# Layer 2's depthwise units: norms with an operand in PSUM, a fourth convolution bank, a sixth half buffer, gate nets in pieces

## The chip, the cores and the metric

The kernel runs on one core of a Trainium2 chip. The metric is the device time of one execution in microseconds, as a median of several runs. The profile that is read here is one further execution, traced instruction by instruction. Engines are called as the profile calls them: PE (TensorE matmul), PEld (its weight load), DVE (VectorE), ACT (ScalarE), POOL (GpSimd), SP (SyncE, here only a DMA queue).

## The reference

The input is x of shape (4, 384, 64, 64), fp32. Four layers follow each other, each as `x = x + layer(groupnorm(x))`: an attention over 96 of the channels, a Fourier filter with a 3x3 depthwise convolution, a re-parametrised depthwise block with a channel MLP, and a 7x7 depthwise convolution with kernels made from the data. The change lies in the third, called layer 2:

```python
p = x.mean(axis=(2, 3), keepdims=True)
h = _gelu(_bn(_pw(p, dc_w1), dc_g1, dc_b1))
decision = jax.nn.sigmoid(_bn(_pw(h, dc_w2), dc_g2, dc_b2))
gate = jax.nn.sigmoid((decision - 0.5) / 1.0)
a = _gelu(_bn(_pw(p, kp_w1), kp_g1, kp_b1))
kw = jax.nn.softmax(_bn(_pw(a, kp_w2), kp_g2, kp_b2), axis=1)
y3 = _bn(_dw(x, c3_w, 1), c3_g, c3_b)
y5 = _bn(_dw(x, c5_w, 2), c5_g, c5_b)
y1 = x * c1_w + c1_b
tok = _bn(kw[:, 0:1] * y3 + kw[:, 1:2] * y5 + y1, ar_g, ar_b)
gp = tok.mean(axis=(2, 3), keepdims=True)
gh = _gelu(_bn(_pw(gp, cg_w1), cg_g1, cg_b1))
gates = jax.nn.sigmoid(_bn(_pw(gh, cg_w2), cg_g2, cg_b2))
tok = tok * gates
h1 = _gelu(_bn(_pw(tok, cm_w1), cm_g1, cm_b1))
h2 = _bn(_pw(h1, cm_w2), cm_g2, cm_b2)
return gate * (tok + h2) + (1.0 - gate) * x
```

`_bn` takes mean and variance over batch and space, `_dw` is a depthwise and `_pw` a 1x1 convolution.

## The kernel before

A tile framework orders the instructions of each engine by its own priorities, gives out the buffers of each pool, and sets the waits. The order in the program text is therefore only roughly the order on an engine, but each engine works through its own list strictly in order.

Layers 0 and 1 run first. Their output x1 goes to DRAM. Then `phase_b` computes the token stage of layer 2 (up to `tok` before its norm), `phase_ef` the gates and the channel MLP, and `phase_g` layer 3.

`phase_b` works in twelve **units** of 32 channels each, with 4 batches x 32 channels on the 128 partitions. A group of four units shares one block of 128 channels of z, the strips of x1 in transposed form: a strip is two image rows (128 positions on the partitions). For each unit:

- `matrices53` makes the banded matrices of the 5x5 and 3x3 convolution for two channels, as a product of taps `w` with a 0/1 band (L1103, tile `toep`, four buffers). Odd ones are made on POOL, with the band in SBUF, and even ones on DVE, with the band in PSUM (`band7_p`).
- `conv53` does the convolution of two channels as six matmuls into one PSUM bank `conv_m` (L1122, three banks). ACT copies it to `d_o` (L1131), DVE takes statistics (L1134), and after every four the ACT queue stores `d_o` to DRAM. There are sixteen of these per unit.
- `conv_norms` turns the statistics into scale and shift of the two batch norms, joined with the branch weights `k_u`: a matmul `cn_rep` for the mean over partitions, small DVE steps for the variance, matmuls `cn_m`, a root as Ln and Exp on ACT (two activation tables), and then some fifteen small DVE steps. It leaves the scales `cn_s`, a shift, and `about`, the point around which squares are summed later.
- `unit_tok` of the unit before runs in the same loop: `c_d` brings the stored convolutions back from DRAM in the other layout, ACT writes `x * c1_w + shift` to the PSUM bank `tok_m` (L1209, two banks), DVE adds the 3x3 and the 5x5 branch (L1212, L1214), ACT sums the squares (L1219), and the SP queue stores `tok`. This is done in four chunks of two halves.
- `unit_strips` of the next unit loads its x1 (`unit_x`, pool `b_x`, two half buffers per unit, five in all), normalises it on ACT (L1044), and, from the second group of four on, transposes it on PE (`strip_m`, L1051) and copies it into z. The first group's strips are made by `strips5`, during layer 1 and at the start of `phase_b`; the last four use `b_x` as well.

Before the units, `nets` computes the gate and the two branch weights from pooled x: two tiny matmuls, each followed by a batch norm over four values (`bn_of_four`: statistics on DVE, Ln and Exp on ACT, three small DVE steps of `bn_scale_shift` at L321 to L323, an activation), and a last pair of matmuls `net_m`. Its instructions are issued before the loop:

```python
self.units(cp)
self.nets(cp)
self.unit_x = [[] for _ in range(UNITS)]
for _ in self.unit_strips(0):
    pass
```

At its start `phase_ef` computes the channel gates, for each of three channel blocks a matmul `cg_z` and a `bn_of_four` with a sigmoid, and then the factors `at` and `ct` that scale every `e_tok` tile ahead of the MLP's first matmul `h_s` (L1342).

PSUM in `phase_b` before: two banks `m` for small results, transposes and `cn_` tiles, one for the band, three `c` for `conv_m`, two `t` for `tok_m`.

Of the kernel before, what the change touches and what calls it, by code (L numbers as in the profile page):

```python
# [39 lines left out]
UNITS = C // 32  # L40
# [185 lines left out]
class _Builder:  # L226
# [728 lines left out]
    def phase_b(self):  # L955

        tc, nc = self.tc, self.nc  # L960
        with ExitStack() as ctx:
            self.open_psum(ctx, 2)
            cp = ctx.enter_context(tc.tile_pool(name="b_const", bufs=1))
            self.bx_p = ctx.enter_context(tc.tile_pool(name="b_x", bufs=5))
            self.bt_p = ctx.enter_context(tc.tile_pool(name="b_t", bufs=2))
            self.bc_p = ctx.enter_context(tc.tile_pool(name="b_c", bufs=3))
            self.band7 = self.const(cp, "band7")
            self.band7_p = self.psum.tile([P, 512], F32, tag="band", name="band7_p", bufs=1)[:, 0:W]
            nc.vector.tensor_copy(self.band7_p, self.band7)
# [12 lines left out]
            for _ in self.unit_strips(0):  # L982
                pass
            for u in range(UNITS):
                st = self.bt_p.tile([P, 2, 16, 6], F32, tag="st", name="st")
                strips = self.unit_strips(u + 1) if u + 1 < UNITS else iter(())
                tok = self.unit_tok(u - 1) if u else iter(())
                for n in range(16):
                    self.matrices53(16 * u + n + 2)
                    self.conv53(u, n, st)  # L990
                    next(strips if n % 2 else tok, None)
                self.conv_norms(u, st)
            for _ in self.unit_tok(UNITS - 1):
                pass
            self.tok_stats()

    def units(self, pool):

        nc = self.nc
        self.norm_u = pool.tile([P, 3, UNITS], F32, tag="norm_u", name="norm_u")  # L1000
        self.same32 = self.const(pool, "same32")
        self.swap(
            self.norm_u.rearrange("p k (j q) -> p (k j) q", q=4), self.norm2.rearrange("p k j b -> p (k j) b")
        )

# [3 lines left out]
        self.k_u, self.about = tile_of("k_u", 2), tile_of("about", UNITS)  # L1009
# [101 lines left out]
    def conv53(self, u, n, st):  # L1111

        nc = self.nc
        c0 = u % 4 * 32 + 2 * n
        t = self.toep.pop(16 * u + n)
        if n % 4 == 0:
            self.d_o = self.bt_p.tile([P, 2, 8, P], F32, tag="d_o", name="d_o")
        m = self.psum.tile([P, 512], F32, tag="c", name="conv_m", bufs=3)
        for c in range(2):
            for i in range(3):  # L1120
                at = (c0 + c) * 132 + 4 * i
                nc.tensor.matmul(  # L1122
                    m[:, c * 256 : (c + 1) * 256],
                    lhsT=self.z_[:, at : at + P],
                    rhs=t[:, 12 * c + 4 * i : 12 * c + 4 * i + 4].rearrange("p m a n -> p (m a n)"),
                    start=i == 0,
                    stop=i == 2,
# [14 lines left out]
    def conv_norms(self, u, st):  # L1142


        nc = self.nc
        at = slice(u, u + 1)
        parts = st.rearrange("p v n (e s) -> p (v n e) s", e=2)
        rep = self.pm("cn_rep")
        nc.tensor.matmul(rep[:, 0:64], lhsT=self.mean128, rhs=parts[:, :, 1], start=True, stop=True)
# [23 lines left out]
        c = self.sm([P, 2], "cn_c")  # L1173
        s = self.sm([P, 2], "cn_s")
        for v, k in enumerate(("c5", "c3")):
            nc.vector.tensor_mul(a[:, v : v + 1], a[:, v : v + 1], self.vec(f"{k}_g")[:, at])
        nc.vector.tensor_mul(c, mean, a)
        s0 = self.sm([P, 1], "cn_s0")
        nc.vector.tensor_copy(s0, self.vec("c1_b")[:, at])
        for v, k in enumerate(("c5", "c3")):  # L1180
            nc.vector.tensor_sub(c[:, v : v + 1], self.vec(f"{k}_b")[:, at], c[:, v : v + 1])
            nc.vector.scalar_tensor_tensor(s0, c[:, v : v + 1], self.k_u[:, v : v + 1], s0, ALU.mult, ALU.add)
        nc.vector.tensor_mul(s, a, self.k_u)

        about = self.about[:, at]
        nc.vector.tensor_add(about, self.c1_u[:, at], s0)
        nc.vector.tensor_mul(mean, mean, s)
        for v in range(2):
            nc.vector.tensor_add(about, about, mean[:, v : v + 1])
        nc.vector.tensor_scalar(about, about, -1.0, None, ALU.mult)  # L1190
        self.tok_s = s, s0

    def unit_tok(self, u):
# [4 lines left out]
        for i in range(4):  # L1198
# [40 lines left out]
    def nets(self, cp):  # L1239
# [8 lines left out]
            nc.tensor.matmul(z[0:12, 0:B], lhsT=w1[:, j, :], rhs=self.p2[:, j, :], start=j == 0, stop=j == NJ - 1)  # L1248
        hid = self.sm([12, B], "net_h")
        self.bn_of_four("net1", z[0:12, 0:B], self.vec("net_g1", 12), self.vec("net_b1", 12), AF.Gelu, hid)  # L1250
        z = self.pm("net_z2")
        nc.tensor.matmul(z[0:3, 0:B], lhsT=w2, rhs=hid, start=True, stop=True)
        z2 = self.sm([3, B], "net_z2s")
        self.bn_of_four("net2", z[0:3, 0:B], self.vec("net_g2", 3), self.vec("net_b2", 3), AF.Identity, z2)

        m = self.pm("net_m")
        nc.tensor.matmul(m[:, 0:B], lhsT=net[:, 0:P], rhs=z2, start=True, stop=True)
# [10 lines left out]
        for v, k in enumerate((self.k5, self.k3)):  # L1268
            nc.vector.tensor_mul(own, k, self.vec("batch"))
            nc.vector.tensor_reduce(self.k_u[:, v : v + 1], own, AX.X, ALU.add)  # L1270

    def phase_ef(self):
        tc, nc = self.tc, self.nc
        with ExitStack() as ctx:
# [30 lines left out]

# [479 lines left out]
```

## Time and profile before

| | |
|---|---|
| time, median of 3 | 5168.03 us (5156.67 to 5169.5) |
| span of the profiled run | 5165.3 us, mean granted clock 0.947 |
| PE busy | 4669.4 us, 90% |
| DVE busy | 2742.2 us, 53% |
| ACT busy | 2093.9 us, 41% |
| POOL busy | 734.3 us, 14% |
| first to last matmul of L1122 | 2628.4 to 3258 us |
| first matmul of the MLP, `h_s` | 3311.0 us |

A group row of the profile gives busy time, the mean of one instruction, and the idle time before it with what ended it. The view of waits says which instruction waited for which, in total. The view of stretches gives the busy time of every engine between two times, the granted clock (1.00 is full speed), the share of the 16 DMA engines and the rate. The timeline lists instructions in order of time, with the idle time ahead of each in square brackets. Every fp32 matmul appears as two records.

### The profile page before, as it was taken

How to read it: one execution, taken by the hardware profiler on the slowest of the kernel's cores; microseconds unless marked ns; L12 is line 12 of the kernel's file. 1: busy time of each engine (PE TensorE's matmuls, PEld its weight loads, DVE VectorE, ACT ScalarE, POOL GpSimd, SP SyncE). 2: the span in 40 equal slices, each digit the busy share in tenths (PEclk: the TensorE clock that was granted, in tenths of full speed). 3: DMA queues.
4: the chain of work that ended last, by engine and by line, in shares of the span. 5: the costliest groups of instructions: out<-in, count | busy, mean ns of one | idle time of the engine just before them, and what ended most of it. 6: DMA issues, size and time to landing. Idle time of an engine off the chain costs nothing. (4 is left out here: it accounts for less than half of the span.)

```text
span 5165.3 us, 48069 instructions
## 1 busy us (share of the span) xinstructions
PE 4669.4 (90%) x17963; PEld 2579.1 (50%) x17963; DVE 2742.2 (53%) x4606; ACT 2093.9 (41%) x2736; POOL 734.3 (14%) x524
## 2 busy tenths in 40 slices
PE   5999999999999999999878999599999995549999
PEld 2333444334443343435457777344444442449999
DVE  4322456634565345566768888644431113657775
ACT  3544344454444444433135555411133334652320
POOL 1000000000000000000035555100000000125433
PEclk9999999999999999999979999799999997659999
DMA  5210211111121111112158999766644434647776
GB/s 157 74 48 28 88 56 67 55 54 45 49 74 66 36 37 63 66 68 93 65 161 259 271 279 278 250 242 240 250 175 164 155 134 173 225 169 245 228 223 190
DMA packets 387543, 723.30 MB, mean 140 GB/s; under 512 B 21627, under 2 KB 221158, under 8 KB 380390
## 3 DMA queue, kind: packets, MB, share of 16 engines
q1 hardware_dynamic: 333528, 519.50, 32.4%
q10 hardware_dynamic: 28494, 105.99, 5.2%
q0 software_dynamic: 25280, 94.65, 4.7%
q8 instruction: 145, 2.38, 0.2%
q14 instruction: 96, 0.79, 0.0%
HBM read 432.48 MB, written 287.57 MB: 139 GB/s over the span
## 5 line engine op out<-in xcount | busy, mean ns | idle before, releaser
L734 PE MATMUL av<-probs,vt 128*97 128x512 f32 x2048 | 962.2, 605 | 0.0
L703 ACT ACTIVATE probs<-sc_s 128x1024 f32<-128x1024 f32 x512 | 499.5, 1021 | 756.6 <-PE av L734 739.5
L734 PEld LDWEIGHTS av<-probs,vt 128*97 128x97 f32 x2048 | 322.1, 166 | 507.7 <-issue 504.3
L1122 PE MATMUL conv_m<-toep,z 128*128 128x256 f32 x2304 | 527.4, 389 | 33.5 <-ACT d_o L1131 17.6
L918 DVE SCALAR_TENSOR_TENSOR acc<-band,vecs,acc 128x512 f32<-128x512 f32 x696 | 493.1, 746 | 42.6 <-POOL band L879 25.0
L1391 PE MATMUL h_m<-f_h,cm_w_t 128*128 128x512 f32 x1152 | 496.2, 594 | 7.9 <-ACT f_h L1381 7.9
L1122 PEld LDWEIGHTS conv_m<-toep,z 128*128 128x128 f32 x2304 | 443.0, 195 | 98.9 <-issue 17.7
L1103 POOL TENSOR_TENSOR toep<-w,band 128x1536 f32<-128x1536 f32 x96 | 330.4, 3442 | 313.3 <-PE conv_m L1122 254.3
L1342 PE MATMUL h_s<-e_tok,cm_w_t 128*128 128x512 f32 x768 | 366.4, 601 | 5.1 <-DVE e_tok L1327 5.1
L1675 PE MATMUL conv_m<-toep,z 128*128 128x128 f32 x3072 | 364.7, 277 | 1.9 <-DVE rest_o L1683 1.9
L1391 PEld LDWEIGHTS h_m<-f_h,cm_w_t 128*128 128x128 f32 x1152 | 219.7, 191 | 284.4 <-issue 271.7
L1675 PEld LDWEIGHTS conv_m<-toep,z 128*128 128x128 f32 x3072 | 355.7, 194 | 2.4 <-issue 2.1
L695 PE MATMUL sc_s<-q,k 32*128 32x512 f32 x2048 | 300.8, 644 | 16.3 <-ACT probs L703 11.5
L841 PE MATMUL t_m<-w_in_t,xb 128*128 128x384 f32 x768 | 283.6, 503 | 7.6 <-DVE coef L858 3.3
L767 PE MATMUL proj_m<-xm,w_proj_t 128*128 128x512 f32 x576 | 265.8, 600 | 0.8 <-DVE xm L720 0.8
L1349 ACT COPY e_h<-h_s 128x1024 f32<-128x1024 f32 x96 | 97.2, 1012 | 415.8 <-PE h_s L1342 415.8
L774 DVE SCALAR_TENSOR_TENSOR x_res<-proj_m,bn_c,x_res 128x512 f32<-128x512 f32 x96 | 71.8, 748 | 338.0 <-PE proj_m L767 338.0
L1342 PEld LDWEIGHTS h_s<-e_tok,cm_w_t 128*128 128x128 f32 x768 | 148.2, 193 | 191.9 <-issue 185.5
L1351 DVE BATCH_NORM_STATS2 h_st<-e_h 128x6 f32<-128x512 f32 x192 | 123.4, 685 | 203.7 <-ACT e_h L1349 203.7
L1399 DVE BATCH_NORM_STATS2 h_st<-f_h 128x6 f32<-128x512 f32 x72 | 50.0, 694 | 322.8 <-ACT f_h L1398 322.8
L841 PEld LDWEIGHTS t_m<-w_in_t,xb 128*128 128x128 f32 x768 | 142.3, 193 | 151.0 <-issue 66.3
L1342 PE MATMUL h_s<-z,cm_w_t 128*128 128x512 f32 x384 | 198.3, 600 | 12.6 <-DVE z L1327 12.6
(366 smaller groups left out, 6322.5 us busy)
## 6 DMA issues: line engine op xcount, KB each, us to landing
d<-d_o ACTq DMA_DIRECT2D x96, 512.0 KB
c_d<-d SPq DMA_DIRECT2D x96, 512.0 KB
hid<-e_h ACTq DMA_DIRECT2D x16, 3072.0 KB
f_h<-hid SPq DMA_DIRECT2D x16, 3072.0 KB
x_res<-in_x SPq DMA_DIRECT2D x32, 768.0 KB
x_in<-in_x SPq DMA_DIRECT2D x96, 256.0 KB
xa<-x_res POOLq DMA_DIRECT2D x32, 768.0 KB, 3.9
xa_in<-xa SPq DMA_DIRECT2D x32, 768.0 KB
```

Source lines behind the costliest of these rows:

```text
L695: nc.tensor.matmul(s[:, g], lhsT=k4[32 * g : 32 * g + 32, c], rhs=q[i][32 * g : 32 * g + 32], start=True, stop=True,)
L703: nc.scalar.activation(p[:, h * 1024 : (h + 1) * 1024], s[:, 2 * h : 2 * h + 2].rearrange("p a b -> p (a b)"), AF.Exp, scale=0.25,)
L734: nc.tensor.matmul(av[0 : PD + 1, :], lhsT=vt[:, 4 * c + v, :], rhs=p[:, v * 512 : (v + 1) * 512], start=c == 0 and v == 0, stop=c == 7 an ...
L767: nc.tensor.matmul(m, lhsT=self.w_proj[:, j, o * P : (o + 1) * P], rhs=xm[:, j], start=j == 0, stop=j == NJ - 1,)
L841: nc.tensor.matmul(m[:, 0:C], lhsT=xb[:, j], rhs=self.w_in[:, j, :], start=j == 0, stop=j == NJ - 1,)
L918: nc.vector.scalar_tensor_tensor(out, src(j, k), w, done, ALU.mult, ALU.add)
L1103: eng.tensor_tensor(t, self.w53[:, at : at + 192].rearrange("p (m n) -> p m n", n=8).unsqueeze(2).to_broadcast([P, 24, 8, 8]), band.rearra ...
L1122: nc.tensor.matmul(m[:, c * 256 : (c + 1) * 256], lhsT=self.z_[:, at : at + P], rhs=t[:, 12 * c + 4 * i : 12 * c + 4 * i + 4].rearrange("p ...
L1342: nc.tensor.matmul(s[:, v, :], lhsT=w1[:, j, o * P : (o + 1) * P], rhs=t[j][:, v * 512 : (v + 1) * 512], start=j == 0, stop=j == NJ - 1,)
L1351: nc.vector.bn_stats(st[:, o, 8 * b + 2 * i + v, :], h[:, o, v * 512 : (v + 1) * 512])
L1391: nc.tensor.matmul(m, lhsT=w2[:, o, j * P : (j + 1) * P], rhs=h[:, o, v * 512 : (v + 1) * 512], start=o == 0, stop=o == 5,)
L1675: nc.tensor.matmul(m[:, ch * P : (ch + 1) * P], lhsT=self.z_[:, at : at + P], rhs=t[:, 8 * c + 2 * i : 8 * c + 2 * i + 2].rearrange("p m a ...
```

## The change

Five things change, all in layer 2:

1. `conv_norms`: the mean and its deviation stay in PSUM (`rep`, `m`), so that each two-input DVE step has at most one operand in SBUF. A copy (`cn_four`) and a square go to ACT. The products of gains and biases with the branch weights, for all units at once, are made in `nets` (`gk`, `base`), as is `about`, which needs no convolution statistics after all since the means cancel. The small DVE steps from the root to the shift and to `about`, some fifteen, become four.
2. `conv_m` gets four banks, `tok_m` one. The last unit's `tok_m` uses the four `c` banks, which are free then.
3. `b_x` gets a sixth half buffer.
4. `nets` becomes a generator in pieces, taken up after the third, sixth and ninth convolution of unit 0, and unit 0's own `unit_strips` moves into that loop.
5. The gates of `phase_ef` are normed for all three channel blocks together, with one root.

```diff
-            self.bx_p = ctx.enter_context(tc.tile_pool(name="b_x", bufs=5))
+            self.bx_p = ctx.enter_context(tc.tile_pool(name="b_x", bufs=6))
...
-            self.nets(cp)
             self.unit_x = [[] for _ in range(UNITS)]
-            for _ in self.unit_strips(0):
-                pass
...
-                tok = self.unit_tok(u - 1) if u else iter(())
+                tok = self.unit_tok(u - 1) if u else self.unit_strips(0)
+                nets = iter(()) if u else self.nets(cp)
                 for n in range(16):
                     self.matrices53(16 * u + n + 2)
                     self.conv53(u, n, st)
                     next(strips if n % 2 else tok, None)
+                    if n % 3 == 2:
+                        next(nets, None)
...
-        m = self.psum.tile([P, 512], F32, tag="c", name="conv_m", bufs=3)
+        m = self.psum.tile([P, 512], F32, tag="c", name="conv_m", bufs=4)
...
-        rep = self.pm("cn_rep")
-        nc.tensor.matmul(rep[:, 0:64], lhsT=self.mean128, rhs=parts[:, :, 1], start=True, stop=True)
-        d = self.sm([P, 64], "cn_d")
-        nc.vector.tensor_sub(d, parts[:, :, 1], rep[:, 0:64])
-        nc.vector.tensor_mul(d, d, d)
-        nc.vector.scalar_tensor_tensor(d, parts[:, :, 2], 1.0 / P, d, ALU.mult, ALU.add)
...
-        nc.vector.tensor_copy(four[:, 0], spread(parts[:, :, 1]))
+        nc.scalar.copy(four[:, 0], spread(parts[:, :, 1]))
+        rep = self.pm("cn_rep")
+        mean, d = rep[:, 0:64], rep[:, 64:128]
+        nc.tensor.matmul(mean, lhsT=self.mean128, rhs=parts[:, :, 1], start=True, stop=True)
+        nc.vector.tensor_sub(d, parts[:, :, 1], mean)
+        nc.scalar.activation(d, d, AF.Square)
+        nc.vector.scalar_tensor_tensor(d, parts[:, :, 2], 1.0 / P, d, ALU.mult, ALU.add)
...
-        mean = self.sm([P, 2], "cn_mean")
-        nc.vector.tensor_copy(mean, m[:, 0:2])
-        a = self.sm([P, 2], "cn_a")
-        self.rsqrt(a, m[:, 2:4])
...
-        about = self.about[:, at]
-        nc.vector.tensor_add(about, self.c1_u[:, at], s0)
-        nc.vector.tensor_mul(mean, mean, s)
-        for v in range(2):
-            nc.vector.tensor_add(about, about, mean[:, v : v + 1])
-        nc.vector.tensor_scalar(about, about, -1.0, None, ALU.mult)
+        self.rsqrt(m[:, 4:6], m[:, 2:4])
+        nc.vector.tensor_mul(s, m[:, 4:6], self.gk[:, u])
+        nc.vector.tensor_mul(m[:, 6:8], m[:, 0:2], s)
+        nc.vector.scalar_tensor_tensor(s0, m[:, 6:7], -1.0, self.base[:, u : u + 1], ALU.mult, ALU.add)
+        nc.vector.scalar_tensor_tensor(s0, m[:, 7:8], -1.0, s0, ALU.mult, ALU.add)
...
-                m = self.psum.tile([P, 512], F32, tag="t", name="tok_m", bufs=2)
+                last = u == UNITS - 1
+                m = self.psum.tile([P, 512], F32, tag="c" if last else "t", name="tok_m", bufs=4 if last else 1)
...
+            z = self.pm("cg_z2")[:, 0 : NJ * B].rearrange("p (j b) -> p j b", b=B)
+            mv = self.sm([P, NJ, 2], "cg2_mv")
             for j in range(NJ):
-                z = self.pm("cg_z2")
-                nc.tensor.matmul(z[:, 0:B], lhsT=cg2[:, j * P : (j + 1) * P], rhs=gh, start=True, stop=True)
+                nc.tensor.matmul(z[:, j], lhsT=cg2[:, j * P : (j + 1) * P], rhs=gh, start=True, stop=True)
+                st = self.sm([P, 6], "cg2_st")
+                nc.vector.bn_stats(st, z[:, j])
+                nc.vector.bn_aggr(mv[:, j], st)
+            ga, gc = self.bn_scale_shift("cg2", mv[:, :, 0], mv[:, :, 1], self.vec("cg_g2"), self.vec("cg_b2"))
+            for j in range(NJ):
                 gates = self.sm([P, B], "gates")
-                self.bn_of_four(
-                    "cg2", z[:, 0:B], self.vec("cg_g2")[:, j : j + 1], self.vec("cg_b2")[:, j : j + 1], AF.Sigmoid, gates
-                )
+                nc.scalar.activation(gates, z[:, j], AF.Sigmoid, bias=gc[:, j : j + 1], scale=ga[:, j : j + 1])
```

More of the change, by code (lines that the diff above doesn't have):

```diff
@@ L1008, in units @@
         tile_of = lambda name, *n: pool.tile([P, *n], F32, tag=name, name=name)
-        self.k_u, self.about = tile_of("k_u", 2), tile_of("about", UNITS)
+        self.k_u, self.gk = tile_of("k_u", 2), tile_of("gk", UNITS, 2)
+        self.base, self.about = tile_of("base", UNITS), tile_of("about", UNITS)
         self.total, self.squares = tile_of("tok_sum", UNITS, 8), tile_of("tok_sq", UNITS, 4)
@@ L1145, in conv_norms @@
         nc = self.nc
-        at = slice(u, u + 1)
         parts = st.rearrange("p v n (e s) -> p (v n e) s", e=2)
-        rep = self.pm("cn_rep")
-        nc.tensor.matmul(rep[:, 0:64], lhsT=self.mean128, rhs=parts[:, :, 1], start=True, stop=True)
-        d = self.sm([P, 64], "cn_d")
-        nc.vector.tensor_sub(d, parts[:, :, 1], rep[:, 0:64])
-        nc.vector.tensor_mul(d, d, d)
-        nc.vector.scalar_tensor_tensor(d, parts[:, :, 2], 1.0 / P, d, ALU.mult, ALU.add)
         four = self.bt_p.tile([P, 2, 2, B, 32], F32, tag="cn_four", name="cn_four", bufs=1)
         spread = lambda t: t.rearrange("p (v c) -> p v c", v=2).unsqueeze(2).to_broadcast([P, 2, B, 32])
-        nc.vector.tensor_copy(four[:, 0], spread(parts[:, :, 1]))
+        nc.scalar.copy(four[:, 0], spread(parts[:, :, 1]))
[5 more added lines that the diff above has]
+        nc.vector.scalar_tensor_tensor(d, parts[:, :, 2], 1.0 / P, d, ALU.mult, ALU.add)
         nc.vector.tensor_copy(four[:, 1], spread(d))
@@ L1168, in conv_norms @@
                 )
-        mean = self.sm([P, 2], "cn_mean")
-        nc.vector.tensor_copy(mean, m[:, 0:2])
-        a = self.sm([P, 2], "cn_a")
-        self.rsqrt(a, m[:, 2:4])
-        c = self.sm([P, 2], "cn_c")
         s = self.sm([P, 2], "cn_s")
-        for v, k in enumerate(("c5", "c3")):
-            nc.vector.tensor_mul(a[:, v : v + 1], a[:, v : v + 1], self.vec(f"{k}_g")[:, at])
-        nc.vector.tensor_mul(c, mean, a)
         s0 = self.sm([P, 1], "cn_s0")
[L1179 to L1183, printed above, removed]
-        about = self.about[:, at]
-        nc.vector.tensor_add(about, self.c1_u[:, at], s0)
-        nc.vector.tensor_mul(mean, mean, s)
-        for v in range(2):
-            nc.vector.tensor_add(about, about, mean[:, v : v + 1])
-        nc.vector.tensor_scalar(about, about, -1.0, None, ALU.mult)
+        self.rsqrt(m[:, 4:6], m[:, 2:4])
[3 more added lines that the diff above has]
+        nc.vector.scalar_tensor_tensor(s0, m[:, 7:8], -1.0, s0, ALU.mult, ALU.add)
         self.tok_s = s, s0
@@ L1250, in nets @@
         self.bn_of_four("net1", z[0:12, 0:B], self.vec("net_g1", 12), self.vec("net_b1", 12), AF.Gelu, hid)
+        yield
         z = self.pm("net_z2")
@@ L1254, in nets @@
         self.bn_of_four("net2", z[0:3, 0:B], self.vec("net_g2", 3), self.vec("net_b2", 3), AF.Identity, z2)
+        yield
         m = self.pm("net_m")
@@ L1270, in nets @@
             nc.vector.tensor_reduce(self.k_u[:, v : v + 1], own, AX.X, ALU.add)
+        nc.vector.tensor_copy(self.base, self.vec("c1_b"))
+        for v, k in enumerate(("c5", "c3")):
+            kv = self.k_u[:, v : v + 1]
+            nc.vector.tensor_scalar(self.gk[:, :, v], self.vec(f"{k}_g"), kv, None, ALU.mult)
+            nc.vector.scalar_tensor_tensor(self.base, self.vec(f"{k}_b"), kv, self.base, ALU.mult, ALU.add)
+        nc.vector.scalar_tensor_tensor(self.about, self.c1_u, -1.0, self.base, ALU.mult, ALU.subtract)
+        yield
     def phase_ef(self):
```

## The prediction

> **What bounds the kernel now.** The slices of the page show TensorE at 9 tenths almost everywhere and lower in slices 21 to 24 and around 25. The change touches only the stage that lies there (the units of layer 2, 2628 to 3258 us) and the gate nets right behind it, so I cut that stage into its twelve units with the view of stretches. A unit is cut where its `cn_rep` matmul starts.
>
> ```profile
> 2628.40:2685.40 57.00, 49.40 (x210) 41.88 (x207) 32.64 (x68) 26.96 (x40) 25.40 (x8) 0.91 0.48 141
> 2685.40:2740.40 55.00, 47.53 (x210) 41.20 (x210) 47.91 (x85) 26.03 (x39) 28.85 (x9) 0.94 0.81 244
> 2740.40:2786.40 46.00, 41.90 (x190) 36.02 (x188) 35.07 (x77) 25.27 (x39) 26.20 (x9) 0.96 0.96 290
> 2786.40:2848.10 61.70, 51.94 (x234) 44.20 (x235) 48.04 (x88) 31.18 (x48) 28.96 (x9) 0.92 0.80 235
> ...
> 2899.70:2951.30 51.60, 47.26 (x235) 40.85 (x235) 42.18 (x87) 29.68 (x46) 27.55 (x9) 1.00 0.91 275
> ...
> 3209.20:3257.60 48.40, 44.95 (x202) 38.70 (x202) 40.14 (x88) 23.45 (x38) 21.34 (x7) 0.96 0.86 268
> ```
>
> Columns: length, busy PE, PE weight load, DVE, ACT, POOL, granted clock, DMA share, GB/s. TensorE leads in every unit (DVE is at 42.2 of 51.6, ACT at 29.7), and units 4 to 10 are alike. The work in a unit is 16 convolutions of 2.59 us (spacing of the `d_o` copies in an undisturbed stretch) = 41.4, in units 3 to 10 also 32 transposes of 0.109 = 3.5, and about 1.1 for the norms' matmuls: 42.5 or 46.0 us. What is above that is waiting and slow clock. Who it waits for, TensorE alone, over the stage:
>
> ```profile
> PE conv_m L1122 <- ACT d_o L1131: 17.6, 9, 5.6
> PE strip_m L1051 <- ACT unit_x L1044: 11.7, 8, 1.8
> PE cn_rep L1149 <- DVE st L1134: 8.7, 10, 1.5
> PE conv_m L1122 <- DVE toep L1103: 5.5, 3, 3.2
> PE conv_m L1122 <- DVE about L1189: 5.4, 1, 5.4
> PE net_m L1257 <- ACT net_z2s L349: 4.0, 1, 4.0
> ```
>
> Each row: us in total, times, longest. The first wait is one per unit; I followed it back in the timeline of unit 8:
>
> ```profile
> 3067.03 3.44 POOL L1103 TENSOR_TENSOR toep<-w,band 128x1536 f32<-128x1536 f32 x1 [2.20 <-PE conv_m L1122]
> ...
> 3067.91 2.57 DVE L1189 TENSOR_TENSOR about<-about,cn_mean 128x1 f32<-128x1 f32 x1
> ...
> 3074.29 1.15 ACT L1219 ACTIVATE c_d<-c_d,about 128x1024 f32<-128x1024 f32 x1 [5.63 <-DVE c_d L1214]
> ...
> 3075.44 0.56 ACT L1131 COPY d_o<-conv_m 128x512 f32<-128x512 f32 x1
> ...
> 3076.15 1.10 PE L1122 MATMUL conv_m<-toep,z 128*128 128x256 f32 x4 [1.50 <-ACT d_o L1131]
> ```
>
> A DVE sum of one element per partition takes 2.57 us: it ends when GpSimd's `toep` product ends (3067.03 + 3.44 = 3070.47). DVE work behind it is late, so ACT stands 5.63 us at the square of L1219 with a `d_o` copy queued behind it, and the matmul that needs that one of three `conv_m` banks starts 1.50 us late. Other copies of the pattern: L1189 takes 3.35 us in unit 1, L1186 3.22 and L1176 2.96 in unit 3, each ending with a GpSimd product. So the chain is GpSimd, DVE, ACT, TensorE.
>
> **What the Trainium skill says.** (1) SBUF — State Buffer, Who interferes with whom: a DVE instruction with two SBUF inputs shares a read path with a GpSimd instruction reading SBUF, and one waits for the other's whole length; with one SBUF input it does not. The trace agrees: the sums above are held to GpSimd's end, while DVE's own `toep` product, whose band lies in PSUM, keeps 1.745 us beside it. (2) TensorE: Matmul & The Clock Gate, What's actually happening: after about 3.4 us idle the array runs at half clock until it has been busy as long. The trace shows it from shorter gaps too: 122 records (twelve to a convolution, so 0.216 us each) after the 5.59 us gap took 28.07 us where 26.4 are due (1.7 lost), 96 after a 2.00 us gap lost 1.9; after 1.50 us none is lost. (3) PSUM — Partial Sum Buffer, Specifications (TRN2): eight banks. The stage uses all of them (2 small, 1 band, 3 `conv_m`, 2 `tok_m`), so the fourth `conv_m` bank is taken from `tok_m`. No run shows the number itself.
>
> **The change part by part.**
>
> *1. Norms.* Per unit DVE loses the cn_d square 0.23, a `cn_four` copy 0.33, and in the tail of the chain the copies and sums of L1170 to L1190, about 2.3 us unheld, plus holds of up to 3.35; it gains four small ones (0.15 to 0.22 each). All that remain have a PSUM operand, so none is held. ACT gains a 128x256 copy (between its 128x128 row, 0.298, and its 128x512 row, 0.583: 0.4) and a 128x64 square (row L1706: 0.345). ACT has 22 us free per unit. The square adds a trip DVE to ACT to DVE before the variance matmuls; those stand four to six convolution matmuls behind `cn_rep` (1.7 us and more), which hides it in steady units.
>
> *2. Steady units 4 to 10.* Their gaps are 0.24 + 0.72 + 0.46 + 1.50 + 1.41 = 4.33. I laid the new engine orders over the measured durations of unit 8. Exp ends near 3062.3 instead of 3064.96, the first `tok_m` runs about 1 us earlier, the square no longer meets a held sum, and with four banks no conv waits for `d_o`: 1.50 goes. The scaling of `unit_x`, which ACT did late for the same reason, now ends about 0.4 after TensorE wants it instead of 1.41. The other three sit between the last statistics, the transposes and the next unit; their order is the same, and they stay. Saving 2.5 x 7 = 17.5; a unit comes to 49.1.
>
> *3. The single `tok_m` bank.* This is the added wait: ACT's next `tok_m` (0.78) waits for DVE's second sum (L1214), and `d_o` copies queue behind it; DVE then waits for ACT. One half costs 0.78 + 0.74 + 0.74 + handovers of about 0.07, some 2.45; eight are 19.6 of a 49 us unit, so no bound. In the new order DVE has statistics, a `toep` or a z copy between most pairs, 0.8 to 1.7 us, as long as ACT needs. Cost taken: 0; at most 0.5 per half, 4 per unit, were nothing hidden.
>
> *4. Unit 3.* Pure 46.0, took 61.7, with 5.39 (about), 1.81 (unit_x), 1.29 and 4.1 of slow clock. With the holds gone I take the steady gaps 1.8 plus 3 for late `c_d` loads: 51, saving 10.7.
>
> *5. Units 0 to 2 and nets.* They took 158.0 for 3 x 42.5 plus net matmuls 1.6 = 129. Lost: net_m 4.0, and behind it DVE `toep` 3.2 (its weights came late, because SyncE's queue stood 23.3 us at a `unit_x` load until the first `d_o` store, which the nets held back), 5.59, 2.00, and slow clock after each. The nets now stand after convs 3, 6 and 8, so ACT and DVE answer while conv matmuls run, and the sixth `b_x` buffer lets the first unit's loads pass. New loss: unit 0's `cn_rep` and mean matmuls now follow its last conv directly; `d_o` copy, statistics, two `unit_x` scalings on ACT and the `cn_four` copy give 2 to 4 us idle and 1.7 of slow clock. With a net wait of 0 to 4 (L323 is still SBUF with SBUF, held 3.16 before; I take 2), 5.4 at that border and 2.5 for the rest: 139, saving 19 (12 to 25).
>
> *6. Unit 11* loses its 1.5 gap: 1.5. *Behind it*, 53.4 us without matmul work: first `c_d` landing (3267.6), its fourth pair (3281.3) and the gate weights (3300) are DMA and keep their distance, so the extra banks for the last `tok_m` save about 0.6.
>
> *7. Gates.* Three norms with table loads of 1.283 become one. The third gate's factors were ready at 3317.3, and TensorE, started at 3311.0 with the first two, stood again until 3318.9. Now all are ready near 3311 to 3313, and the same four products end about 2 us sooner: 2.
>
> Sum: 17.5 + 10.7 + 19 + 1.5 + 0.6 + 2 = 51.3. 5168 - 51 = 5117.
>
> **Rivals.** *A, DMA takes over.* A unit moves 275 x 51.6 = 14.2 MB; unit 2 ran at 290 GB/s with a share of 0.96, so about 302 at full share, 47.0 us. 49.1 needs 289 GB/s, 0.96 again, and loads that land late would stall ACT at a square. For it: the 3.8 us that DVE waited for `c_d` in unit 1. Against: no `c_d` wait in units 4 to 10, where the queue has idle stretches (share 0.32 at 3020 to 3024). If steady units stop at 50.3 (9 saved) and units 0 to 3 save 19 of 30, with 4 elsewhere: 32, 5136. *B, the `tok_m` bank gives the steady gain back*: 0 there, the rest stays as priced less 7: 27, 5141. *C, slower*: 0.5 per half unhidden is 4 per unit, 44 in eleven units, with the steady gain gone and half of the rest, 17, kept: 27 slower, 5195; the slack of four banks speaks against it. *D, no wait at the unit 0 border and none at the nets, unit 3 like a steady one*: 7 + 2 + 6 more, 5102.
>
> **How the numbers follow.** Forecast 0.55, A 0.22, B 0.08, D 0.10, slower 0.02, within 0.3% 0.03. The range 5095 to 5143 takes in A, B and D with the before's own spread (5157 to 5170). Faster by over 0.3% (under 5152.5): 0.95; same 0.03; slower 0.02.
>
> **What would show each step.** In the profile after: no tiny DVE sum of the norms over 0.3 us; waits of conv for `d_o` under 3 us in all (17.6 before); units 4 to 10 near 49 us with `unit_x` waits under 0.6; a gap of 2 to 4 us at unit 0's `cn_rep`; `net_m` wait under 4; the stage 576 to 585 us (629 before). Wrong if units 4 to 10 stay above 50.5, if ACT's `tok_m` waits for the second sum show up as conv waits, or if rows waiting for DMA `c_d` appear.

## The result, and the profile after

The changed kernel takes 5126.93 us (median; 5123.52 to 5139.64), the kernel before, on the same chip, 5162.35. The ratio is 0.9937, with a 95% interval of 0.9911 to 0.9962: 0.6% faster, some 33 to 35 us where 51 were forecast. That the total came within 10 us of the forecast 5117 all the same is in part luck: beside it the kernel before took 5162 us, not the 5168 that the forecast started from.

The view of stretches of the changed kernel, cut at the starts of `cn_rep` as before (length, busy PE, PE weight load, DVE, ACT, POOL, granted clock, DMA share, GB/s), for units 0 to 3, a steady unit and unit 11:

```profile
2620.10:2673.60 53.50, 45.81 (x204) 38.58 (x204) 35.08 (x71) 25.72 (x38) 25.34 (x8) 0.94 0.44 131
2673.60:2727.50 53.90, 50.25 (x221) 43.62 (x221) 39.43 (x71) 28.46 (x42) 29.71 (x9) 0.94 0.91 276
2727.50:2772.50 45.00, 40.55 (x184) 35.01 (x184) 32.08 (x67) 25.68 (x41) 25.38 (x8) 0.96 0.91 281
2772.50:2829.20 56.70, 50.88 (x234) 43.48 (x235) 41.10 (x75) 32.03 (x50) 29.05 (x9) 0.94 0.86 261
2925.60:2973.80 48.20, 46.80 (x234) 40.98 (x234) 38.48 (x74) 30.47 (x48) 27.56 (x9) 1.00 0.97 297
3166.70:3213.30 46.60, 44.70 (x202) 38.80 (x202) 37.07 (x76) 24.39 (x40) 21.29 (x7) 0.96 0.85 270
```

Worked out from these starts:

| stretch | before | after | forecast |
|---|---|---|---|
| units 0 to 2 | 158.0 | 152.4 | 139 |
| unit 3 | 61.7 | 56.7 | 51 |
| each of units 4 to 10 | 51.6 | 48.2 | 49.1 |
| unit 11 | 48.4 | 46.6 | 46.9 |
| stage, first convolution to `cn_rep` of unit 11 | 629.2 | 593.2 | 576 to 585 |
| from there to the second product of `h_s` | 61.2 | 59.7 | 2.6 less |

The stage gave 36.0 us and the gates 1.5. The steady units gave more than forecast (23.8 for 17.5), the first four much less (10.6 for 29.7). The profiled spans differ by 43.5, but 8.3 of that arose ahead of the stage, in code that the change doesn't touch (the first convolution starts anywhere between 2619 and 2634 us over the traces of this study). So the experiments are compared by the length of the stage, with the timed median beside it.

TensorE's waits in the stage after (us in total, times, longest):

```profile
PE cn_rep L1154 <- DVE st L1135: 11.3, 12, 1.5
PE conv_m L1123 <- DVE toep L1104: 8.3, 6, 3.0
PE net_m L1246 <- ACT net_z2s L349: 4.0, 1, 4.0
PE conv_m L1123 <- DVE z L1057: 3.6, 8, 0.5
PE cn_m L1163 <- ACT cn_four L1151: 2.5, 1, 2.5
PE strip_m L1052 <- ACT z L1059: 1.9, 8, 0.2
PE strip_m L1052 <- ACT unit_x L1045: 1.8, 1, 1.8
```

The 17.6 us for `d_o` and the 5.4 for `about` are gone, and `unit_x` fell from 11.7 to 1.8. The wait at `net_m` is the same 4.0 as before, and a wait for `cn_four` is new. Both lie at unit 0. One row of DVE's waits in the stage is new as well, since DVE waited for no `c_d` there before:

```profile
DVE tok_m L1199 <- DMA c_d<-d: 8.7, 6, 3.0
```

The first of the two at unit 0, in the timeline:

```profile
2642.05 3.40 POOL L1104 TENSOR_TENSOR toep<-w,band 128x1536 f32<-128x1536 f32 x1 [2.14 <-PE conv_m L1123]
2642.07 3.40 DVE L323 TENSOR_TENSOR net_c<-vecs,net_c 3x1 f32<-3x1 f32 x1
2645.50 0.35 ACT L349 ACTIVATE net_z2s<-net_z,net_c,net_a 3x4 f32<-3x4 f32 x1 [4.05 <-DVE net_c L323]
...
2645.90 0.58 PE L1246 MATMUL net_m<-net_z2s,net 3*128 3x4 f32 x2 [3.99 <-ACT net_z2s L349]
...
2648.91 17.59 PE L1123 MATMUL conv_m<-toep,z 128*128 128x256 f32 x72 [2.00 <-DVE toep L1104]
```

The shift of the second net, one number on three partitions, has both operands in SBUF and ends with GpSimd's product. TensorE waits at `net_m`, then 2.0 more for a product that DVE could not begin, and the 72 records after it take 17.59 where 15.55 are due: 8.0 in all. ("Due" is 0.216 us a record. A row ends some 0.25 later than that gives, 16 undisturbed records show 3.72 for 3.46, so the slow clock's part here is nearer 1.8.) The second wait, at the border of units 0 and 1:

```profile
2673.64 0.45 PE L1154 MATMUL cn_rep<-st,mean 128*128 128x64 f32 x2 [1.47 <-DVE st L1135]
2673.76 2.37 ACT L1045 ACTIVATE unit_x<-unit_x,norm_u 128x1024 f32<-128x1024 f32 x2 [0.96 <-ACT d_o L1132]
...
2676.04 0.52 ACT L1151 COPY cn_four<-st 128x256 f32<-128x256 f32 x1
...
2676.61 1.01 PE L1163 MATMUL cn_m<-mean,cn_four 128*128 128x1 f32 x4 [2.51 <-ACT cn_four L1151]
...
2677.48 2.91 PE L1123 MATMUL conv_m<-toep,z 128*128 128x256 f32 x6
```

`cn_rep` stands directly behind unit 0's last convolution, the `cn_four` copy behind two scalings of `unit_x` on ACT. TensorE loses 1.47 + 2.51, and then runs at a slow clock (six records in 2.91, undisturbed 1.54).

A loss of another kind lies in the middle of unit 2. DVE, then TensorE, in the changed kernel:

```profile
2746.11 0.76 DVE L1135 BATCH_NORM_STATS2 st<-d_o 128x6 f32<-128x256 f32 x2 [2.15 <-ACT d_o L1132]
2746.79 3.40 DVE L1104 TENSOR_TENSOR toep<-w,band_p 128x1536 f32<-128x1536 f32 x2
...
2748.67 22.38 PE L1123 MATMUL conv_m<-toep,z 128*128 128x256 f32 x96 [3.00 <-DVE toep L1104]
```

DVE stands 2.15 us for the copy of a convolution's result, whose statistics its list has ahead of two products in a row. TensorE has used up the products by then and waits 3.00.

### The profile page after: what moved, and what is told of

Read it like the earlier page. It is cut to its first block, busy times and chain, and to the rows that moved or that the text cites. A ratio compares the mean times of both kernels' runs of the same rounds, so it can differ in the third digit from the quotient of the medians.

```text
span 5121.8 us, 47956 instructions
## 1 busy us (share of the span) xinstructions
PE 4654.7 (91%) x17963; PEld 2568.2 (50%) x17963; DVE 2696.9 (53%) x4450; ACT 2098.7 (41%) x2753; POOL 734.2 (14%) x524
## 5 line engine op out<-in xcount | busy, mean ns | idle before, releaser
L918 DVE SCALAR_TENSOR_TENSOR acc<-band,vecs,acc 128x512 f32<-128x512 f32 x696 | 492.8, 745 | 42.6 <-POOL band L879 25.0
L841 PEld LDWEIGHTS t_m<-w_in_t,xb 128*128 128x128 f32 x768 | 140.8, 191 | 147.7 <-issue 64.3
```

The source lines that it names most:

```text
L841: nc.tensor.matmul(m[:, 0:C], lhsT=xb[:, j], rhs=self.w_in[:, j, :], start=j == 0, stop=j == NJ - 1,)
L918: nc.vector.scalar_tensor_tensor(out, src(j, k), w, done, ALU.mult, ALU.add)
```

## The experiments

These are all the runs, with one trace each. "By `cn_rep`" are the lengths of units from the starts of `cn_rep`, as the forecast cut them. "Place" is the number of matmul records of the next unit (twelve to a convolution, 0.216 us each) that TensorE's list has ahead of the `cn_rep` of units 0 / 1 / 2.

Where the place differs, this cut lies elsewhere in the work: 18 records are 3.9 us. So the column "by convolutions" has the same units from the first record of their first convolution to that of the next unit, 192 records each, counted in the traces. Only this one compares single units between runs; what TensorE waits behind a unit's last convolution is in that unit.

"Steady" is the usual length. Two things vary from trace to trace by themselves: the clock at which unit 0 starts and recovers (some 3 us), and single steady units that take 1.7 us more (up to two in a trace; e3, which swings, apart). Differences of the stage under some 4 us are not read.

| run | median us | ratio to before (95%) | units 0, 1, 2, 3 by `cn_rep` | by convolutions | steady | stage | place |
|---|---|---|---|---|---|---|---|
| before | 5162.35 | 1 | 57.0, 55.0, 46.0, 61.7 | 55.3, 53.7, 50.7, 60.9 | 51.6 | 629.2 | 8 / 14 / 0 |
| after | 5126.93 | 0.9937 (0.9911 to 0.9962) | 53.5, 53.8, 45.1, 56.7 | 57.4, 44.8, 52.0, 55.8 | 48.2 | 593.2 | 0 / 18 / 0 |
| e1 norms only | 5119.43 | 0.9919 (0.9893 to 0.9944) | 55.7, 43.9, 42.5, 56.2 | 53.9, 42.6, 47.3, 55.4 | 48.5 | 584.6 | 8 / 14 / 0 |
| e2 banks back | 5129.82 | 0.9930 (0.9902 to 0.9958) | 53.8, 50.9, 46.2, 54.6 | 57.5, 45.0, 50.1, 53.7 | 48.5 | 591.8 | 0 / 10 / 0 |
| e3 five half buffers | 5156.41 | 0.9981 (0.9972 to 0.9989) | 55.1, 52.4, 46.8, 59.9 | 58.9, 44.8, 48.4, 64.3 | 47.6 to 53.2 | 616.0 | 0 / 14 / 10 |
| e4 nets, strips ahead | 5107.96 | 0.9886 (0.9862 to 0.9911) | 55.7, 43.0, 45.2, 46.0 | 54.0, 42.6, 42.6, 51.7 | 48.2 | 575.9 | 8 / 10 / 18 |
| e5 strips ahead | 5115.95 | 0.9907 (0.9890 to 0.9923) | 59.8, 43.0, 44.6, 46.0 | 58.1, 42.6, 42.6, 51.0 | 48.2 | 579.1 | 8 / 10 / 18 |
| e6 nets ahead | 5127.26 | 0.9938 (0.9921 to 0.9954) | 53.9, 48.3, 47.5, 56.7 | 56.4, 44.1, 50.9, 55.8 | 48.2 | 590.5 | 0 / 6 / 0 |
| e7 as e4, banks back | 5107.22 | 0.9891 (0.9874 to 0.9907) | 58.5, 43.9, 41.7, 49.2 | 56.8, 42.6, 42.6, 52.2 | 48.5 | 578.3 | 8 / 14 / 10 |
| e8 as e5, free shift | 5118.17 | 0.9909 (0.9892 to 0.9925) | 58.8, 43.0, 45.1, 47.7 | 57.0, 42.6, 42.6, 53.2 | 48.2 | 580.2 | 8 / 10 / 18 |
| e9 as e4, free shift | 5098.97 | 0.9887 (0.9858 to 0.9915) | 49.8, 43.0, 44.7, 47.6 | 48.0, 42.6, 42.6, 52.7 | 48.2 | 569.2 | 8 / 10 / 18 |
| e10 as e9, gate weights first | 5094.61 | 0.9872 (0.9842 to 0.9901) | 51.7, 43.0, 44.6, 46.0 | 49.9, 42.6, 42.6, 51.0 | 48.2 | 567.8 | 8 / 10 / 18 |
| e11 as e9, weights on ACT's queue | 5123.37 | 0.9919 (0.9888 to 0.9950) | 44.7, 48.9, 50.4, 58.0 | 47.2, 44.7, 53.8, 57.2 | 48.2 | 587.7 | 0 / 6 / 0 |
| e12 norms later | 5115.45 | 0.9909 (0.9890 to 0.9928) | 51.6, 42.6, 47.9, 54.6 | 49.0, 42.6, 52.3, 53.7 | 48.2 | 582.5 | 12 / 12 / 0 |

**e1, the norms alone.** The new `conv_norms` and its tables in the kernel before; all else as before.

> The kernel before with the new norms alone: three convolution banks, two for tok_m, five half buffers, nets ahead of the loop, gates as before. The stage (first convolution to the cn_rep of unit 11) took 629.2 us before and 593.2 with the whole change; a steady unit (4 to 10) 51.6 and 48.2. Theory N (the norms' release from GpSimd is the whole steady gain, the fourth bank only slack): steady units 48.2 to 48.6, the waits of convolutions for d_o under 3 us in all, stage 600 to 606. Theory B (the fourth bank is what lets the d_o copies be late): the d_o wait of 1.5 per unit stays, steady units 49.5 to 50.2, stage 612 to 618.

The stage is 584.6 us: the norms alone bring 44.6, more than the whole change. A steady unit takes 48.5 with three banks, and no convolution waits for `d_o`. Theory B falls, and N was too timid: units 1 and 2 gain 14.6 as well. So the rest of the change costs 8.6 us in the stage; the medians of the two kernels can't be told apart. e1 takes away norm steps on DVE as well as their holds, and which of the two brings how much was not tested apart.

**e2, the banks alone undone.**

```diff
-        m = self.psum.tile([P, 512], F32, tag="c", name="conv_m", bufs=4)
+        m = self.psum.tile([P, 512], F32, tag="c", name="conv_m", bufs=3)
...
-                m = self.psum.tile([P, 512], F32, tag="c" if last else "t", name="tok_m", bufs=4 if last else 1)
+                m = self.psum.tile([P, 512], F32, tag="t", name="tok_m", bufs=2)
```

> The changed kernel with three banks for conv_m and two for tok_m again. Theory N (the single tok_m bank costs nothing and the fourth bank brings nothing): stage within 2 us of 593.2, steady units 48.2. Theory B (the fourth bank is needed): d_o waits come back, steady units 49 or more, stage 599 or more. Theory S (the single tok_m bank makes ACT wait for DVE, with d_o copies and so statistics and toep products behind it, and this is what units 1 to 3 lost): units 1 to 3, 155.6 us together in the changed kernel, shorten by 4 to 8, and the 3.0 us wait for toep in unit 2 goes. Theory D (late landings of c_d cost units 1 to 3): they stay within 1.5 us.

591.8 against 593.2: N, but for the steady units at 48.5. Units 1 to 3 are 3.9 shorter, within the spread. The 3 us waits for `toep` stay (7.9 us in all, the longest 3.1), so the single `tok_m` bank did not make them, and no `d_o` wait returns. The banks change a steady unit by 0.3. Theory D is out by other traces: in e6 and e12 neither DVE nor ACT waits more than 0.2 us for `c_d` in units 0 to 3, and the loss is there; in e7 DVE waits 11.2 us for it there, and the loss is not.

**e3, five half buffers** (`bufs=5` at `b_x`).

> The changed kernel with five half buffers of x1. If the sixth buffer only serves unit 0 (the weights of the products queue behind a load that waits for a buffer): unit 0 is 2 to 5 us longer, steady units stay at 48.2, stage 595 to 598. If it also serves the steady units (their wait for unit_x went from 1.41 to 0, more than forecast): steady units 48.6 to 49.6, stage 598 to 607. If neither: stage within 1 us of 593.2.

616.0 us, beyond both ends. With the strips in the loop, five buffers let the steady units swing between 47.6 and 53.2 us, and TensorE waits 11.4 us for `unit_x` and 11.6 for `toep` over the stage. The same five buffers gave an even 48.5 in e1, with the strips ahead. Why they matter only in the one order was not followed up.

**e4, nets and first strips ahead of the loop.**

```diff
+            for _ in self.nets(cp):
+                pass
             self.unit_x = [[] for _ in range(UNITS)]
+            for _ in self.unit_strips(0):
+                pass
...
-                tok = self.unit_tok(u - 1) if u else self.unit_strips(0)
-                nets = iter(()) if u else self.nets(cp)
+                tok = self.unit_tok(u - 1) if u else iter(())
```

> The changed kernel with the nets and the first unit's strips issued ahead of the loop, as before. The forecast put up to 12 us on this part together with the sixth buffer; the trace shows the wait of net_m at 4.0 us in both kernels, since the shift of the second net is held by GpSimd in both. If the pieces bring what was forecast: stage 600 or more, with a wait for toep of 3 us and one for d_o of 4 us or more back in unit 0. If they only moved the wait: stage within 3 us of 593.2.

The stage shortens by 17.3 us to 575.9, where both answers had it equal or longer. By their convolutions units 0 to 3 gain 3.4, 2.2, 9.4 and 4.1. (Of the 10.8 and 10.7 that units 1 and 3 gain by `cn_rep`, 3.5 and 3.9 are the cut that moved.) Unit 0 starts with a slow clock here (its first 16 records take 5.88, undisturbed 3.72). TensorE's timeline at the border of units 0 and 1:

```profile
2665.91 22.68 PE L1124 MATMUL conv_m<-toep,z 128*128 128x256 f32 x104 [3.22 <-DVE toep L1105]
2688.44 0.36 PE L1155 MATMUL cn_rep<-st,mean 128*128 128x64 f32 x2
2688.63 2.80 PE L1124 MATMUL conv_m<-toep,z 128*128 128x256 f32 x12
2691.26 0.50 PE L1164 MATMUL cn_m<-mean,cn_four 128*128 128x1 f32 x4
```

No brackets behind the first row: `cn_rep` comes eight records into unit 1's first convolution, and TensorE neither waits nor slows down. In unit 2 DVE's products now come one at a time, and no convolution waits for one:

```profile
2745.85 1.75 DVE L1105 TENSOR_TENSOR toep<-w,band_p 128x1536 f32<-128x1536 f32 x1
...
2750.31 1.75 DVE L1105 TENSOR_TENSOR toep<-w,band_p 128x1536 f32<-128x1536 f32 x1
```

**e5 and e6, which of the two.** e5 takes only the strips ahead of the loop, e6 only the nets.

> The changed kernel with the first unit's strips (loads and scalings of x1) ahead of the loop again, the gate nets still in pieces inside it. With both ahead the stage was 575.9 us against 593.2, unit by unit 55.7, 43.0, 45.2, 46.0 against 53.5, 53.8, 45.1, 56.7. Theory Q (the strips in the loop do the harm: the norms of unit 0 then stand directly behind its last convolution, and SyncE's loads come in a worse order): units 1 to 3 fall to 134 to 137 and unit 0 stays at 52 to 55, stage 571 to 577. Theory P (the nets' pieces do it): units 1 to 3 stay at 150 to 156, stage 588 to 594.

> The changed kernel with the gate nets ahead of the loop and the first unit's strips in it. Theory Q: a stall of 4 us and more between the last convolution of unit 0 and the next one, units 1 to 3 at 148 to 156, stage 588 to 597. Theory P: units 1 to 3 at 134 to 140, stage 574 to 580.

Theory Q holds in that the strips do the harm: units 1 to 3 take 133.6 us with them ahead and 152.5 with them in the loop (by convolutions 136.2 and 150.8), wherever the nets stand (136.9 in e4, 152.6 in the changed kernel). Part 4 mixed a harmless edit with a harmful one. But unit 0 of e5 missed its range (59.8). First SyncE's list, then TensorE's, in e5:

```profile
2613.02 37.78 SPq L1040 DMA_DIRECT2D unit_x<-x  x12
2653.17 0.83 SPq L1093 DMA_DIRECT2D w<-in_c_t  x2
...
2667.90 24.12 PE L1125 MATMUL conv_m<-toep,z 128*128 128x256 f32 x104 [10.44 <-DVE toep L1106]
```

The taps for convolutions 8 to 11 stand behind twelve `unit_x` loads on the queue, and TensorE waits 10.4 us for the product of convolution 8. Moving the strips into the loop did cure that (that wait is 2.0 in the changed kernel), and paid for it at the border behind unit 0 and in units 2 and 3.

**e7, which buffer helps.** e4 with the edit of e2.

> Norms, six half buffers and gates of the change; nets and first strips ahead of the loop; three banks for conv_m, two for tok_m. The norms alone left unit 3 at 56.2 us, where norms with four banks and six buffers had it at 46.0. If the sixth buffer did that: unit 3 at 46 to 48, stage 575 to 579, steady units 48.2 to 48.5. If the fourth bank did it: unit 3 at 54 to 57, stage 583 to 588.

Unit 3 takes 49.2, between the two, but its cut has moved. By convolutions units 2 and 3 together take 102.7 us in e1, 94.8 in e7 and 94.3 in e4: the sixth buffer takes off 7.9 there, and the fourth bank brings nothing that can be told. The first answer holds. In the medians neither can be told from the next run.

**e8 and e9, the held shift.** Scale and shift of the small norms by operations with one tensor operand:

```diff
-        a, c = self.bn_scale_shift(name, mv[:, 0:1], mv[:, 1:2], g, b)
+        a = self.sm([parts, 1], f"{name}_a")
+        c = self.sm([parts, 1], f"{name}_c")
+        self.rsqrt(a, mv[:, 1:2])
+        nc.vector.tensor_scalar(a, a, g, None, ALU.mult)
+        nc.vector.tensor_scalar(c, mv[:, 0:1], a, b, ALU.mult, ALU.subtract)
+        nc.vector.tensor_scalar(c, c, -1.0, None, ALU.mult)
```

> The kernel of the first run of this set with the scale and shift of the small norms worked out by operations of one tensor operand (the other two as one number per partition), where the shift of net 2 had two operands in SBUF and was held 3.4 us to the end of GpSimd's product. If that hold is what makes TensorE wait 4.0 us at net_m and then 2 to 3 us for the toep product behind it: the shift takes 0.2 us, both waits go, unit 0 falls by 5 to 9 us to 45 to 49, stage 564 to 570. If ACT's table loads in the net's chain make the wait: net_m's wait stays above 2 us and unit 0 falls by less than 3.

e8 missed, and could not tell. In e5 GpSimd was itself waiting for taps when the shift ran, so the wait at `net_m` was already 0.7. It is 0.9 in e8, and the 10.4 us for `toep` hide the rest. e9 puts the edit into e4, where the shift was held 3.16 us:

> The kernel with nets and first strips ahead of the loop (unit 0: 55.7 us, of it 4.0 waiting at net_m, 3.2 for a toep product whose weights were late, the rest slow clock), with the scale and shift of the small norms by operations of one tensor operand. If the 3.4 us hold of the shift makes the wait at net_m: the shift takes under 0.3 us, net_m waits 1 us or less. If the late weights follow from it too (ACT, held up by the net, issues the first d_o store late, and SyncE's queue stands at a load until then): the wait for toep falls under 1.5 us and unit 0 to 46 to 50, stage 566 to 571. If the weights come at their own time: the wait for toep grows by what net_m gives back, unit 0 at 53 to 56, stage 574 to 577.

GpSimd's product and the shift's steps in e9, then `net_m`:

```profile
2625.81 3.44 POOL L1110 TENSOR_TENSOR toep<-w,band 128x1536 f32<-128x1536 f32 x1 [13.44 <-issue]
...
2628.31 0.25 DVE L352 TENSOR_SCALAR net_c<-net_mv,net_a,vecs 3x1 f32<-3x1 f32 x1
...
2630.78 0.38 PE L1252 MATMUL net_m<-net_z2s,net 3*128 3x4 f32 x2
```

The shift takes 0.25 us while GpSimd's product runs, `net_m` waits for nothing, and unit 0 falls by 5.9 to 49.8. Of that, 2.2 is a faster clock at its start; e10, which starts as slowly as e4, has 51.7, the 4.0 of the wait less. So the hold made that wait; in e10 to e12, which have the edit too, `net_m` waits for nothing either. The wait for `toep` stays at 3.2, as neither answer said: product and matmul moved forward together.

**e10, the gap behind the stage.** The two `cg_w` loads stand ahead of the two `cm_w` loads on ACT's queue.

> The same with the two small weights of the gates behind the stage loaded before the two large ones on ACT's queue. Behind unit 11's cn_rep TensorE stood 54 to 56 us until the first h_s, 12 to 15 of it at cg_z for the gate weights. If these weights set the end of that gap: 6 to 12 us less (first h_s 44 to 49 us behind that cn_rep). If the large weights or the tok loads set it: under 3 us less.

The queue of ACT and what follows, in the changed kernel:

```profile
3242.31 0.82 ACTq L281 DMA_DIRECT2D cm_w_t<-in_cm_w_t  x2
3243.18 9.15 ACTq L281 DMA_DIRECT2D cg_w_t<-in_cg_w_t  x2
3252.35 1.28 ACT L311 ACT_TABLE_LOAD   x1 [12.05 <-DMA cm_w_t<-in_cm_w_t]
```

and in e10:

```profile
3219.09 1.20 ACTq L281 DMA_DIRECT2D cg_w_t<-in_cg_w_t  x2
3220.32 0.84 ACTq L281 DMA_DIRECT2D cm_w_t<-in_cm_w_t  x2
3221.20 1.28 ACT L311 ACT_TABLE_LOAD   x1 [4.12 <-DMA cg_w_t<-in_cg_w_t]
```

Issuing the small loads behind the large ones took 9.15 us of ACT's own list, with the norm of `tok` queued behind (9.54 in e9, but 2.10 in the kernel before, so the order alone doesn't set it). The first `h_s` now comes 47.3 us behind unit 11's `cn_rep`, not 56.8 (e9); e12, with the same order, has 48.2. At 5094.61 us this is the fastest kernel of the study. Its interval and that of the changed kernel don't overlap. That it beats e9 is shown in this gap, not in the medians, whose intervals do overlap.

**e11 and e12, the place of the norms.** e11 is e9 with this:

```diff
-            self.nc.sync.dma_start(self.w53_ahead, src.rearrange("p c t n v -> p (c t n v)"))
+            queue = self.nc.scalar if n in (8, 12) else self.nc.sync
+            queue.dma_start(self.w53_ahead, src.rearrange("p c t n v -> p (c t n v)"))
```

> The kernel of the first run of this set with two of the loads of c53 weights (for convolutions 8 to 15) on ACT's queue, where no load of x1 stands ahead of them. The scheduler then puts the cn_rep of unit 0 and of unit 2 directly behind their last convolution, as in the changed kernel, where with the loads on SyncE it lets 4 to 9 matmuls of the next unit go first. If that place makes the stall between units: 4 us and more of waits and 2 to 3 of slow clock are back between units 0 and 1, unit 1 at 48 to 54, stage no better than 575. If only late loads made it: units 1 to 3 stay at 134 and unit 0 falls under 48, stage 564 to 570.

The first answer. Unit 0 falls to 44.7 (its matmul work is 43.0), but its norms are back directly behind it:

```profile
2672.45 0.45 PE L1161 MATMUL cn_rep<-st,mean 128*128 128x64 f32 x2 [1.47 <-DVE st L1142]
2673.07 0.61 PE L1170 MATMUL cn_m<-mean,cn_four 128*128 128x1 f32 x4 [0.17 <-ACT cn_four L1158]
2674.98 5.46 PE L1130 MATMUL conv_m<-toep,z 128*128 128x256 f32 x12 [1.30 <-DVE toep L1111]
```

The waits are 2.9 us, fewer than the 4 expected, and the slow clock adds 2.7 (twelve records in 5.46, undisturbed 2.80). Units 1 to 3 take 157.3 (by convolutions 155.7, 137.9 in e9). e12 adds to e10 only the load for convolutions 8 to 11 on ACT's queue, and writes the norms one convolution later:

```diff
                     self.conv53(u, n, st)
+                    if n == 0 and u:
+                        self.conv_norms(u - 1, last)
...
-                self.conv_norms(u, st)
+                last = st
```

> The kernel of run e10 with one load of c53 weights (convolutions 8 to 11) on ACT's queue, and with the norms of a unit written behind the first convolution of the next. The scheduler now puts the cn_rep of units 0 and 1 one whole convolution into the next unit; that of unit 2 stays directly behind its last convolution. In run e11 the early weights brought unit 0 to 44.7 us, and units 1 to 3 to 48.9, 50.4 and 58.0. If the place of cn_rep at unit 0 starts that loss: unit 0 at 44 to 48 (its last convolution is 2.6 later than in e11), unit 1 at 43, unit 2 at 41 to 45, unit 3 at 46 to 50, stage 560 to 567, total 5081 to 5093. If the order in which loads land makes it, wherever cn_rep stands: units 1 to 3 at 150 and more, stage 580 or more.

A miss for both answers. Unit 0 took 51.6 (49.0 by convolutions), since a 3.2 us wait for a product is back, now at convolution 12, whose taps are on SyncE's queue. Unit 1 is at 42.6 and TensorE waits no more than 0.6 at that border, so the place at unit 0 does make the loss there. Units 2 and 3 still lose, by convolutions 9.7 and 2.7 against e10.

The place at unit 2 goes with that loss: with `cn_rep` directly behind the last convolution, units 2 and 3 together took 102.7 to 111.6 us by convolutions; with the place at 10 or 18 they took 93.6 to 95.8 (e3 with its five buffers apart, 112.7). But in e12 it can't start the loss. The first wait comes at convolution 8 of unit 2 (3.26 us), well ahead of unit 2's `cn_rep`, and as in the changed kernel DVE's list has two products in a row there; so it has in e6 and e11. In e4, e5 and e7 to e10 no convolution of units 1 to 3 waits as much as 0.7 us. So another order on DVE goes with the loss and comes ahead of that place. What sets this order, and whether changing it alone would cure the loss, these runs don't settle.

## Why the prediction was right, and where its sum was off

The direction, the range and the chain of GpSimd, DVE, ACT and TensorE were right. The sum was not: the steady units' 6.3 us more made up for a part of the 19 us that units 0 to 3 gave less. That is luck, since nothing in the forecast tied the two together.

- Step 1 held: no norm step on DVE is held (in a steady unit the longest is the `cn_four` copy, 0.42). The copy on ACT took 0.52 (0.4 estimated), the square 0.21 (0.345).
- Step 2 held, with more: 3.4 us per unit, not 2.5, as the whole 1.41 for `unit_x` went. e1 puts 3.1 of the 3.4 on the norms, e4 against e7 the other 0.3 on the fourth bank. Rival A is out: the steady units run on at 297 GB/s. The sign named for it, rows waiting for `c_d`, did appear (8.7 us), but cost TensorE's steady units nothing: they stayed at 48.2. The 3.8 us cited for A was misread: that wait lies behind unit 11, at 3267.64, not in unit 1. The share given as 0.32 at 3020 to 3024 reads 0.26.
- Step 3 held: the single bank costs nothing (e2). Rival B is out.
- Step 5 failed, by 13.4 of 19 us. Net waits were priced at 2: they measured 8.0, with the hold of L323 in full (4.0), the late product behind it (2.0) and slow clock. The border was priced at 5.4: 1.47 + 2.51 + 3.0 of slow clock made 7.0. The rest was priced at 2.5: 8.4 are left of the 152.4, of it 3.0 waiting for `toep` within unit 2. The prediction saw `cn_rep` of unit 0 move behind its last convolution and charged only that gap, against the gain of letting the taps pass. It did not look at unit 2, nor ask what else moves when the first strips do. That one edit costs 14.6 us with the nets ahead (590.5 less 575.9) and 14.1 with the nets in pieces (593.2 less 579.1).
- Step 4 failed by 5.7 (56.7 for 51), for the most part by the same edit: by its convolutions unit 3 takes 51.0 to 53.2 with the strips ahead (e4, e5, e8 to e10) and 55.8 with them in the loop.
- Step 6 measured 1.8 for unit 11 (3.4 in traces where it doesn't take the 1.7 more); the tail behind it gave nothing that can be told from the landing of loads. Step 7 measured 1.5 for 2: the second stall is gone, the first `h_s` is 2.8 later (56.1 for 53.3). Of that, 1.6 is the gate weights' later landing (`cg_z` 44.1 behind `cn_rep`, 42.5 before); the gates' joint norm keeps the first product waiting for all three.

## What to carry to other kernels

Where an engine that works in order is held by another engine's instruction, look first at the small steps that are held: here the new norms brought 44.6 us, the sixth buffer 7.9 in units 2 and 3 (e1 to e7), and the fourth bank 0.3 in a steady unit. A buffer's worth depends on the order, though: with the strips in the loop, one half buffer less cost 22.8 us (e3). When a scheduler orders the lists, count in the changed lists how much work stands between a reduction's last input and the reduction, at every border and not only at the one edited, and whether work that feeds the critical engine comes in pairs; and undo the parts of a bundle one by one: the best version here leaves part 4 out. When units are compared, cut them at the work and not at an instruction that the scheduler can move. And on an engine that issues DMAs from its own list, put the small load that the next step needs ahead of the large ones.

## What was not expected of the hardware

A DVE operation with one tensor operand, in SBUF, and a constant was held too. In the changed kernel, next to its unheld twin:

```profile
2661.39 0.16 DVE L1314 TENSOR_SCALAR gx<-gx 128x4 f32<-128x4 f32 x1
...
2661.46 3.46 POOL L1104 TENSOR_TENSOR toep<-w,band 128x1536 f32<-128x1536 f32 x1 [1.74 <-PE conv_m L1123]
2661.53 3.42 DVE L1314 TENSOR_SCALAR gx<-gx 128x4 f32<-128x4 f32 x1
```

It ends with GpSimd's product, though it reads one tensor. The prediction's sentence that one SBUF input is safe was too short: the Trainium skill, SBUF — State Buffer, Who interferes with whom, excepts operations that can run in a mode with two ports, and counts those with a tensor and scalars among them. The trace fits that; no run tests it. A `TENSOR_SCALAR` with one element per partition was not held (0.25 us in e9, beside a running product).

The price of a gap is not fixed. After the same wait of 3.2 us in unit 0, the next 104 records took 22.68 us in e4, 24.07 in the kernel before and 25.69 in e7, where 22.46 are due. The Trainium skill, TensorE: Matmul & The Clock Gate, What's actually happening, gives as the reason a window of activity that runs freely; the runs show only the spread. With the 0.25 by which any row ends late, the clock loss after this gap lies between nothing and 3.0, and a forecast should carry both ends.

DMA went further than the prediction's 302 GB/s, in unit 1 of e10:

```profile
2674.60:2717.60 43.00, 43.00 (x205) 37.88 (x205) 35.49 (x68) 26.84 (x40) 27.96 (x9) 1.00 1.02 315
```

TensorE is busy for all of that unit, so this rate did not hold it up.
